# Two places for the maxima over keys, and the value product one step sooner, in a gated cross-attention block on one Trainium2 core

## The chip, the cores and the metric

The kernel runs on 1 core of one Trainium2 chip. The metric is the device time of one execution in microseconds (us). A core has five engines that each work through a queue of their own in order: TensorE (PE in the profile; PEld are its weight loads), VectorE (DVE), ScalarE (ACT), GpSimd (POOL) and SyncE (SP), which here issues most of the DMA transfers. An instruction waits, at the head of its queue, for semaphores that other engines or transfers raise.

## The reference

The inputs are x and a context, 16 x 128 x 1024 in float32 each, two gate scalars and the weights of one block. Cut to what matters:

```python
q = (layernorm(x) @ Wq).reshape(b, s, KV_HEADS, GROUP, HEAD_DIM)      # 8 key heads, groups of 4, 32 wide
k = (ctx @ Wk).reshape(b, s, KV_HEADS, HEAD_DIM)
v = (ctx @ Wv).reshape(b, s, KV_HEADS, HEAD_DIM)
scores = einsum('bqhgd,bkhd->bhgqk', q, k) / sqrt(HEAD_DIM)
out = einsum('bhgqk,bkhd->bqhgd', softmax(scores), v).reshape(b, s, 1024) @ Wo
x = x + tanh(g_xattn) * out
h = silu(layernorm(x) @ W_gate.T) * (layernorm(x) @ W_up.T)           # 2752 wide
x = x + tanh(g_ffn) * (h @ W_down.T)
```

Attention is over the 128 keys of one of the 16 batch elements.

## The kernel before

**Numbers in two parts.** Products are done on pairs of a high part (rounded, type fp32r) and a low part (the rest). `split` makes them: ScalarE copies the source to the high part (line 114), VectorE subtracts it from the source to get the low part (line 115). `mm3` (lines 122 to 124) then multiplies high by high, high by low and low by high.

**The stages.** The 2048 tokens are worked on in two groups of 1024. `projections` makes k, v and q for both groups and writes them to DRAM; `attention` reads them back and works on 64 units per group (one unit is one key head of one batch element: 128 keys against 4 heads x 128 queries, so 512 columns); `Outer` does the product with Wo, the residual and the second layernorm; `Gated` and `Down` are the feed-forward part. The matmuls of these last two are all on line 707.

**Interleaving.** The order is written out by hand: `manual_schedule` keeps each engine's queue in the order in which the program issues. Generators are stepped against each other. The *host* of the first group's attention is `projections`, which yields after every 12 matmuls of 512 columns (about). For each host step `due` grows by RATE = 1.08, and `attention` is stepped once for each whole unit in `due`. So about every twelfth host step is followed by two attention steps at once, a *double step*. The second group's attention runs later with the gated products as its host and has settings of its own.

**One attention step.** With `gap` = 1 a new unit begins at each step. At step i the generator first runs what was put off to this step (`later`: the stores of os, and the reciprocals of the row sums), then in this order `gather`, `scores`, `take`, `rest`, `leave`, `shift`, `expo`, each for unit i minus its lag. The lags of the first group are 0 (scores), 1 (take), 2 (shift), 3 (expo), 4 (rest), 6 (gather), 6 (leave). For unit n they do:
- `scores`, line 472: one matmul into a bank `by` (two places). After every second unit it loads ks and qs for two pairs of units later (lines 451, 465, 466).
- `take`: ScalarE copies the scores to `pr` (line 481, 4 places); GpSimd reduces them to the maximum over the 128 partitions, which are the keys, into `mx` (line 483). `mx` has one place: the pool's default is `bufs=1`.
- `shift`, line 486: VectorE subtracts `mx` from `pr`. It frees `mx`.
- `expo`: ScalarE takes the exponential (line 489) and rounds it to the high part `ph` (line 491, 3 places).
- `rest`, line 495: VectorE makes the low part `pl` = `pr` - `ph` (2 places). It frees `pr`.
- `gather`: two matmuls into a bank `av` (two places), the first with `ph` (line 500), the second with `pl` (line 501). After every second unit it loads the next v (line 458).
- `leave`, line 511: the result goes to `os`, by ScalarE for even units and by VectorE for odd ones, and a step later SyncE stores it (line 515).

The second group calls the same function with nb = 1, lags of its own and another order of the parts.

SyncE's queue holds all of this together with the projections' own transfers: weights (line 168), x (line 218), context (line 188) and the stores of k, v and q (lines 253, 413), in the order of the program.

Of the kernel before, what the change touches and what calls it, by code (L numbers as in the profile page):

```python
# [10 lines left out]
F32 = mybir.dt.float32  # L11
F32R = mybir.dt.float32r
# [5 lines left out]
P = 128  # L18
# [9 lines left out]
TB = 512  # L28
# [26 lines left out]
def flamingo_kernel(ctx: ExitStack, tc: tile.TileContext, x, ctxt, gx, gf, wqkv, wo, wgu, wge, wd, out):  # L55
# [11 lines left out]
    def pool(name, side=None, space=None):  # L67
        kw = {"name": name, "bufs": 1}
        if side:
            kw["side"] = side  # L70
        if space:
            kw["space"] = space
        return tc.tile_pool(**kw)
# [362 lines left out]
    def attention(ap, ps_, cells, gap, lags, npr, nq, nb):  # L436
        units = [(m, j) for m in range(len(cells)) for j in range(2)]
        ks, vs, qs, ss, pr, mx, ph, pl, po = ({} for _ in range(9))
# [40 lines left out]
        def take(n):  # L479
            pr[n] = ap.tile([P, TB], F32, name="pr", tag="pr", bufs=npr)  # L480
            nc.scalar.copy(pr[n], ss.pop(n))  # L481
            mx[n] = ap.tile([P, TB], F32, name="mx", tag="mx")
            nc.gpsimd.partition_all_reduce(mx[n], pr[n], P, bass_isa.ReduceOp.max)  # L483

        def shift(n):
# [1 line left out]

        def expo(n):
            nc.scalar.activation(pr[n], pr[n], AF.Exp, scale=SCALE)
            ph[n] = ap.tile([P, TB], F32R, name="ph", tag="ph", bufs=3)  # L490
            nc.scalar.copy(ph[n], pr[n])

        def rest(n):
# [57 lines left out]
        while i <= last or later:  # L551
            for fn in later.pop(i, []):
                fn()
            for fn in order:
                n = i - steps[fn]
# [17 lines left out]
    class Outer:  # L573
# [38 lines left out]
        def part(self, i, meanwhile=None):  # L612
            raw = self.raw.pop(i)[:, 0]
            self.o[i] = o = stile((i + 1) % 3 if i else 0)
            h, l = (o[:, z].rearrange("p h k t -> p (h k) t") for z in range(2))
            nc.scalar.copy(h, raw)
            if meanwhile:
                meanwhile()
            nc.vector.tensor_tensor(l, raw, f32(h), ALU.subtract)
# [277 lines left out]
    def casts(cb, n):  # L897
        def cast(name, src, k=slice(0, KQ), cols=slice(0, TB)):
            if name not in cb or cb[name] is None:
                cb[name] = mtile(name)  # L900
            c = cb[name]
            kk = slice(k.start, min(k.stop, n))
            split(c[0][:, kk, cols], c[1][:, kk, cols], src[:, kk, cols])

        return cast

    def quarter(mq, i, dtype=F32):

        n = f"q{i // 2}{i % 2}"
        return mq.tile([P, KQ, TB], dtype, name=n, tag=n)  # L910
# [34 lines left out]
    def swap(cb, units, first, mq, n, src, made, early):  # L945

        q = {}

        def load(i, what):
            q[i] = quarter(mq, i)
            nc.sync.dma_start(q[i][:, :n], what())

        def make(name, i):
            cb[name] = None
            casts(cb, n)(name, q[i])

        def bring(name):
            m = cb[name] = mtile(name)  # L960
            for k, z in enumerate(m):
                nc.sync.dma_start(f32(z[:, :n]), made[name][:, k])

        whats = (lambda: src(0, 0), lambda: made["m5"], lambda: src(1, 0), lambda: made["m7"])
        for i, (u, what) in enumerate(zip(early, whats)):
            u.before.append(lambda i=i, what=what: load(i, what))
        u = units[-1]
        u.after[1] = [lambda: (make("m1", 0), load(0, lambda: src(1, 1)))]
        u.after[5] = [lambda: make("m5", 1)]
        u.after[6] = [lambda: bring("m6")]  # L970
        u.after[4] = [lambda: bring("m4")]
        first.after[1] = [lambda: make("m2", 2)]
        first.after[5] = [lambda: make("m7", 3)]
        first.after[6] = [lambda: make("m3", 0)]
# [102 lines left out]
    with ExitStack() as body:  # L1077
        body.enter_context(tc.manual_schedule())
        psB = body.enter_context(pool("psB", None, PSUM))
        cb = {}  # L1080
        o = Outer(0)
        hooks = {
            26: [lambda: o.load(0)],
            28: [lambda: o.added(0)],
            29: [lambda: o.scaled(0)],
            30: [lambda: o.part(0), lambda: o.load(1)],
        }
        with pool("pp", "right") as pp, pool("psP", None, PSUM) as psP:
            pairs = [(t, b) for t in range(2) for b in range(BPB)]
            cells = [(t, c, b) for c in range(2) for t, b in pairs] + [(t, c, b) for t, b in pairs for c in range(2, 4)]  # L1090
            with pool("early", "left") as early:
                host = projections(pp, early, cb, hooks)
                for _ in range(LEAD):
                    next(host)
            with pool("att", "left") as att:
                follow = attention(att, psP, cells, 1, (0, 1, 2, 3, 4, 6, 6), 4, 2, 2)
                due = 0
                for _ in host:
                    due += RATE
                    while due >= 1:  # L1100
                        next(follow, None)
                        due -= 1
                for k, _ in enumerate(follow):
                    if k == 0:
                        o.norm(1)
        mB = body.enter_context(pool("mB", "right"))
        fp = body.enter_context(pool("fp", "right"))
        groups = [[Gated(g, f) for f in range(NFT)] for g in range(NGRP)]
        downs = [[Down(c, p) for p in range(NTOK // (2 * P))] for c in range(len(CHUNKS))]
        tail = groups[1] + sum(downs, [])  # L1110
        for a, b in zip(tail, tail[1:]):
            a.follow = b

        with pool("mq", "left") as mq:
            o.rows(0)
            host = outer(0, cb, lambda: mq, o, groups[0], Edge(0))
            for _ in range(BUSY):
                next(host)
        o = Outer(1)
        with pool("att", "left") as att, pool("psC", None, PSUM) as psC:  # L1120
            cells = [(t, c, b) for t in (2, 3) for b in range(BPB) for c in range(KV // 2)]
            follow = attention(att, psC, cells, 2, (0, 0, 1, 2, 4, 6, 6), 3, 2, 1)
            due, head = 0, len(FIRST) - BUSY
            for k in range(head + 7 * (NFT - 3) + 4):
                due += MORE * (k % 7 == (head + 4) % 7)
                for _ in range(1 + (due >= 1)):
                    next(follow, None)
                due -= due >= 1
                next(host)
            for _ in follow:  # L1130
                pass
        mq = body.enter_context(pool("mq", "left"))
        w = {}

        def fill(z):
            w[z] = quarter(mq, z)
            src = wo[KQ * (z % 2) : KQ * (z % 2) + KQ, :, ts(z // 2, TB)]
            nc.sync.dma_start(w[z], src.rearrange("k p d -> p k d"))

        def turn(z):  # L1140
            cb[QUARTERS[z]] = None
            for k in (0, 2):
                casts(cb, KQ)(QUARTERS[z], w[z], slice(k, k + 2))

        for z in range(4):
            fill(z)
        u = groups[0][-1]
        u.before.append(lambda: (o.rows(0), o.load(0)))
        u.after[5] = [lambda: o.norm(0)]
        u.after[6] = [lambda: turn(0)]  # L1150
        u.after[7] = [lambda: (o.part(0), o.load(1)), lambda: turn(2)]
        u.amid = lambda: turn(1)
        u.after[4] = [lambda: turn(3)]
        for _ in host:
            pass
        for name in ("m1", "m2", "m5"):
            cb[name] = None

        def part(c):
            def src(h, j):  # L1160
                n = len(CHUNKS[c]) // 2
                r = CHUNKS[c][0] * P + h * n * P
                return wd[r : r + n * P, ts(j, TB)].rearrange("(k p) d -> p k d", p=P)

            return src

        before = (groups[1], *downs)
        for c in range(len(CHUNKS)):
            n, made = len(CHUNKS[c]) // 2, {"c": c}
            premake(groups[1][1 + 6 * c :], mq, n, part(c), made)  # L1170
            u = before[c]
            early = (u[-3], u[-3], u[-2], u[-2]) if c == 0 else u[-6:-2]
            swap(cb, u, downs[c][0], mq, n, part(c), made, early)
        for _ in outer(1, cb, lambda: mq, o, tail, Edge(1)):
            pass
# [44 lines left out]
```

## Time and profile before

| | |
|---|---|
| median of 3 runs | 1840.36 us (1840.12 to 1842.83) |
| profiled execution | 1839.81 us, span 1838.0 us |
| TensorE busy | 1816.5 us, 99% of the span |
| VectorE, ScalarE, GpSimd busy | 66%, 49%, 30% |
| first attention, first to last score matmul | 107.1 to 327.7 us |
| GpSimd's maxima (line 483), both groups | 128 of 2157 ns, 276.1 us |
| VectorE's low parts (line 495), both groups | 128 of 945 ns, 121.0 us |

The rows of a timeline are: start in us from the beginning of the span, duration in us, engine, line of the kernel, operation, output <- inputs, and in brackets the idle time of that engine just before and what ended it. A row of waits is: engine, tile and line <- who ended the wait, then us in total, times, longest us. A row on one tile has the shortest, median and longest duration in ns. A row of the stretch table is: window, its length, then busy us (and instructions) of PE, PEld, DVE, ACT, POOL, the granted clock of TensorE, the share of the 16 DMA engines, GB/s.

### The profile page before, as it was taken

To read this page: it belongs to the slowest core of one execution; us is meant where nothing else is said; L and a number is where in the kernel's file an instruction comes from. 1 tells how busy PE (TensorE), PEld (TensorE's weight loads), DVE (VectorE), ACT (ScalarE), POOL (GpSimd) and SP (SyncE) were. 2 spreads that over 40 slices of the span, in tenths; PEclk is the share of its full clock that TensorE was granted. 3 is DMA by queue.
4 is the path that set the end of the run, shared out by engine and by line. 5 is a ranking of instruction groups with operands and counts; after the bars stand their busy time and mean duration, and the time that the engine had idled before them with its cause. 6 is when DMAs were issued, how large, how long until landed. Compare 5 with 4: busy or idle time off the path is not lost.

```text
span 1838.0 us, 23463 instructions
## 1 busy us (share of the span) xinstructions
PE 1816.5 (99%) x8296; PEld 1493.4 (81%) x8296; DVE 1210.6 (66%) x1551; ACT 900.7 (49%) x1301; POOL 546.3 (30%) x372
## 2 busy tenths in 40 slices
PE   9999999999999999999999999999999999999999
PEld 8877877888877777787888888888888888888887
DVE  6758778668877777776578635355356656745765
ACT  4457787435677777776434434333334212312321
POOL 1136566221233333331021233244330231122021
PEclk9999999999999999999999999999999999999999
DMA  9699999774555455543674565675666566665764
GB/s 331 208 274 289 285 285 269 239 258 134 159 146 151 144 148 146 147 138 118 218 252 161 145 204 187 188 210 168 170 206 258 201 233 204 245 215 180 258 201 157
DMA packets 232565, 373.55 MB, mean 203 GB/s; under 512 B 38016, under 2 KB 124288, under 8 KB 227328
## 3 DMA queue, kind: packets, MB, share of 16 engines
q1 hardware_dynamic: 210400, 333.77, 55.7%
q10 hardware_dynamic: 14112, 25.17, 4.6%
q0 software_dynamic: 7936, 13.11, 4.4%
q8 instruction: 66, 1.08, 0.2%
q14 instruction: 51, 0.42, 0.1%
HBM read 247.99 MB, written 122.42 MB: 202 GB/s over the span
## 4 chain that ended last, share of the span: by engine, by line
PE 85%; DVE 5%; DMA 4%; ACT 2%; issue 2%; POOL 1%; SPq 1%; DVEq 0%; POOLq 0%; ACTq 0%
PE bx L707 36%; PE bz L707 18%; PE by L707 9%; PE bz L124 3%; PE bz L122 3%; PE bz L123 3%; PE bx L124 3%; PE bx L123 3%; PE bx L122 3%; PE av L501 1%; DMA od<-os 1%; PE av L500 1%; DVE pl L495 1%; POOL mx L483 1%; DVE pr L486 1%
## 5 line engine op out<-in xcount | busy, mean ns | idle before, releaser
L483 POOL PARTITION_ALL_REDUCE mx<-pr x128 | 276.1, 2157 | 343.4 <-ACT pr L481 167.3
L674 POOL TENSOR_TENSOR sum<-raw 128x512 f32<-128x512 f32 (+1 forms) x37 | 48.0, 1298 | 479.4 <-DVE stc L115 479.4
L114 ACT CAST sta<-raw 128x1024 fp32r<-128x1024 f32 (+1 forms) x66 | 67.7, 1026 | 241.7 <-PE by L707 232.6
L707 PE MATMUL bz<-m5h,stb 128*128 128x512 f32 (+1 forms) x528 | 169.9, 383 | 0.0
L707 PE MATMUL bx<-m4h,std 128*128 128x512 f32 x512 | 168.8, 390 | 1.0 <-DVE c L753 0.8
L707 PE MATMUL bx<-m6h,stb 128*128 128x512 f32 (+1 forms) x528 | 169.6, 383 | 0.0
L707 PE MATMUL bx<-m7h,stc 128*128 128x512 f32 x512 | 168.6, 389 | 0.0
L707 PE MATMUL bz<-m3h,stc 128*128 128x512 f32 x512 | 168.5, 389 | 0.0
L707 PE MATMUL by<-m2h,sta 128*128 128x512 f32 x512 | 168.5, 389 | 0.0
L707 PE MATMUL bx<-m1h,sta 128*128 128x512 f32 x512 | 168.4, 389 | 0.0
L751 DVE TENSOR_TENSOR c<-by,c 128x512 f32<-128x512 f32 x42 | 28.8, 687 | 144.1 <-issue 137.6
L495 DVE TENSOR_TENSOR pl<-pr,ph 128x512 fp32r<-128x512 f32 x128 | 121.0, 945 | 2.2 <-PE av L501 2.2
L144 POOL TENSOR_TENSOR rs__143<-ve,mhalf 128x1 f32<-128x1 f32 x32 | 29.3, 916 | 312.4 <-DVE nm L142 303.0
L851 DVE SCALAR_TENSOR_TENSOR c<-bx,tg,c 128x512 f32<-128x512 f32 x96 | 72.0, 750 | 66.3 <-PE bx L707 62.5
L707 PEld LDWEIGHTS bz<-m5h,stb 128*128 128x128 f32 x528 | 98.2, 188 | 20.2 <-DVE stb L115 0.5
L707 PEld LDWEIGHTS bx<-m6h,stb 128*128 128x128 f32 x528 | 98.4, 188 | 20.0
L707 PEld LDWEIGHTS bx<-m4h,std 128*128 128x128 f32 x512 | 96.1, 188 | 22.6 <-DVE c L753 1.2
L707 PEld LDWEIGHTS bx<-m7h,stc 128*128 128x128 f32 x512 | 96.1, 188 | 20.5 <-issue 0.2
L707 PEld LDWEIGHTS by<-m2h,sta 128*128 128x128 f32 x512 | 96.1, 188 | 20.5
L707 PEld LDWEIGHTS bx<-m1h,sta 128*128 128x128 f32 x512 | 96.1, 188 | 20.4
L707 PEld LDWEIGHTS bz<-m3h,stc 128*128 128x128 f32 x512 | 96.1, 188 | 20.1
L486 DVE TENSOR_TENSOR pr<-pr,mx 128x512 f32<-128x512 f32 x128 | 87.6, 684 | 37.0 <-POOL mx L483 36.7
(400 smaller groups left out, 4635.9 us busy)
## 6 DMA issues: line engine op xcount, KB each, us to landing
raw<-in_wgu SPq DMA_DIRECT2D x42, 1024.0 KB, 6.7
x1d<-c SPq DMA_DIRECT2D x96, 256.0 KB, 2.8
c<-x1d ACTq DMA_DIRECT2D x96, 256.0 KB, 3.0
hd<-c SPq DMA_DIRECT2D x86, 256.0 KB, 2.2
od<-os SPq DMA_DIRECT2D x128, 160.0 KB, 4.0
qd<-e SPq DMA_DIRECT2D x32, 512.0 KB, 5.5
qs<-qd SPq DMA_DIRECT2D x64, 256.0 KB, 4.4
raw<-od SPq DMA_DIRECT2D x32, 512.0 KB, 5.1
```

Source lines behind the costliest of these rows:

```text
L114: nc.scalar.copy(h, src)
L122: nc.tensor.matmul(ps, lh, rh, start=first, stop=False)
L123: nc.tensor.matmul(ps, lh, rl, start=False, stop=False)
L124: nc.tensor.matmul(ps, ll, rh, start=False, stop=last)
L144: nc.gpsimd.tensor_tensor(rs, ve, mhalf, ALU.pow)
L483: nc.gpsimd.partition_all_reduce(mx[n], pr[n], P, bass_isa.ReduceOp.max)
L486: nc.vector.tensor_tensor(pr[n], pr[n], mx.pop(n), ALU.subtract)
L495: nc.vector.tensor_tensor(pl[n], pr.pop(n), f32(ph[n]), ALU.subtract)
L674: lambda: tt(s1, a[1][0], a[1][1], sub),
L707: nc.tensor.matmul(ps, l_, r_, start=start and k == i == 0, stop=k == n - 1 and i == 2, skip_group_check=not start)
L751: tt(c[1], ps, c[1], ALU.add)
L851: nc.vector.scalar_tensor_tensor(y, ps, g, y, ALU.mult, ALU.add)
```

## The change

In the first group (nb = 2) the maxima get two places and the high part `ph` two instead of three. In the second group (nb = 1) both stay as they were. The lags of `gather` and `leave` in the first group go from 6 to 5, so that the value product of unit n stands ahead of the scores of unit n+5 in TensorE's queue, and the copy to os, its store and the next v load move with it.

```diff
         def take(n):
             pr[n] = ap.tile([P, TB], F32, name="pr", tag="pr", bufs=npr)
             nc.scalar.copy(pr[n], ss.pop(n))
-            mx[n] = ap.tile([P, TB], F32, name="mx", tag="mx")
+            mx[n] = ap.tile([P, TB], F32, name="mx", tag="mx", bufs=nb)
             nc.gpsimd.partition_all_reduce(mx[n], pr[n], P, bass_isa.ReduceOp.max)
 ...
         def expo(n):
             nc.scalar.activation(pr[n], pr[n], AF.Exp, scale=SCALE)
-            ph[n] = ap.tile([P, TB], F32R, name="ph", tag="ph", bufs=3)
+            ph[n] = ap.tile([P, TB], F32R, name="ph", tag="ph", bufs=4 - nb)
             nc.scalar.copy(ph[n], pr[n])
 ...
-                follow = attention(att, psP, cells, 1, (0, 1, 2, 3, 4, 6, 6), 4, 2, 2)
+                follow = attention(att, psP, cells, 1, (0, 1, 2, 3, 4, 5, 5), 4, 2, 2)
```

## The prediction

> **What bounds the kernel now.** I read the page first, then TensorE's stretches, then the waits and the timeline of the first attention (100 to 360 us), the only place that the change touches.
>
> ```profile
> PE 1816.5 (99%) x8296; PEld 1493.4 (81%) x8296; DVE 1210.6 (66%) x1551; ACT 900.7 (49%) x1301; POOL 546.3 (30%) x372
> ...
> PE 85%; DVE 5%; DMA 4%; ACT 2%; issue 2%; POOL 1%; SPq 1%; DVEq 0%; POOLq 0%; ACTq 0%
> ```
>
> TensorE (PE) is the bound: work off it counts only where PE stands still. In the timeline, matmuls of 512 columns start 0.227 us apart in a row. What successive starts take beyond that adds up, from 100 to 360 us, to 12.0 us. That is all that can be won. The stretch table shows the worst place:
>
> ```profile
> 270.00:280.00 10.00, 7.54 (x33) 5.41 (x32) 8.32 (x13) 7.26 (x13) 7.30 (x3) 1.00 0.93 290
> 280.00:290.00 10.00, 10.00 (x37) 7.86 (x38) 7.01 (x11) 8.55 (x15) 6.77 (x3) 0.83 0.97 274
> ```
>
> PE is busy 7.54 of 10 us, and in the next row the granted clock (third number from the end) is 0.83. The timeline has the cause, a gap of 2.36 us:
>
> ```profile
> 277.15 0.39 PE L472 MATMUL by<-qs,ks 96*128 96x512 f32 x1
> ...
> 279.91 0.46 PE L500 MATMUL av<-ph,vta 128*80 128x512 f32 x1 [2.36 <-DVE os L511]
> ```
>
> Eight matmuls after it start 0.36 to 0.43 us apart: 1.5 us more. The rest of the 12.0 us: scores that wait for their q load (1.34 us at 178.34, 0.46 at 186.65, 1.04 at 203.57, 1.45 at 213.11), a score that waits for a bank (0.68 at 234.91), and crumbs.
>
> Why the attention is late there: the maxima have one place. Waits of GpSimd (POOL), 100 to 360 us, and a stretch of the timeline, POOL and VectorE (DVE):
>
> ```profile
> POOL mx L483 <- DVE pr L486: 64.4, 51, 5.0
> ```
>
> ```profile
> 257.25 0.67 DVE L486 TENSOR_TENSOR pr<-pr,mx 128x512 f32<-128x512 f32 x1
> ...
> 257.85 1.21 DVE L115 TENSOR_TENSOR wl<-raw,wh 128x1024 fp32r<-128x1024 f32 x1
> ...
> 258.09 3.22 POOL L483 PARTITION_ALL_REDUCE mx<-pr  x1 [1.17 <-DVE pr L486]
> ...
> 258.98 0.68 DVE L495 TENSOR_TENSOR pl<-pr,ph 128x512 fp32r<-128x512 f32 x1
> ...
> 261.34 0.69 DVE L486 TENSOR_TENSOR pr<-pr,mx 128x512 f32<-128x512 f32 x1 [1.68 <-POOL mx L483]
> ```
>
> Each reduce starts 0.17 us after the shift (L486) before it ends, though its input (the copy to pr) lay ready 3.7 us earlier; then DVE stands 1.68 us for the reduce. The two form a ring: reduces start at 254.31, 258.09 and 262.20, so 7.89 us for two units, where PE needs 2 x 3.44 (scores at 248.78, 252.25, 255.69). The ring falls behind by 1 us per pair here.
>
> **The change part by part.** No instruction is added: 64 units keep their counts, and 2 KB per partition go from ph to mx.
>
> *Second place for mx.* The reduce of unit 40 could start when the one before it ends, at 256.92 instead of 258.09. But now shift 39 (due 257.25) runs beside it, which the trace never shows. The nearest row is pl, the same subtraction beside reduces (answers on the tiles mx and ph):
>
> ```profile
> L483 POOL PARTITION_ALL_REDUCE mx<-pr x128: 1783/2080/3220, 111.5 to 848.3; - x128
> ...
> L495 DVE TENSOR_TENSOR pl<-pr,ph x128: 622/684/1573, 120.6 to 860.2; 128x512 fp32r<-128x512 f32 x128
> ```
>
> Its longest is 1573 against 684 ns: 0.89 us lost. So shift 39 ends by 258.8, wl (1.21) and pl (0.68) follow, less overlap, and shift 40 starts at 260.55 instead of 261.34: 0.8 us won per two units. Bounds: 1.68 won (no stretch) to 0.1 lost (two stretches of 0.89). I take 0.8. It matters where the 1.68 waits stand: units 10, 12, 14, 16, 20 and 34, 36, 38, 40, 42, 44, 46.
>
> [...]
>
> *Value product a step sooner.* The value pair (L500, L501) of unit n stands ahead of score n+5 instead of n+6. Its second matmul needs pl of n, which DVE makes in attention step n+4. PE reaches it 0.23 us before the old start of score n+5, plus 0.46 us since one more pair (2 x 0.23) has been issued. Against the ends of pl in the trace, what is too late (with 0.06 us for the signal) is largest at unit 6 (142.60 against 140.91: 1.75 us) and unit 41 (272.50 against 270.13: 2.43). Behind a standing pair on PE's queue wait the next score and 12 projection matmuls.
>
> Worst are the five places where two attention steps follow each other without projections, because pl then has no time between (second scores 9, 22, 36, 49, 63). There units 4, 17, 31, 44, 58 are late by 1.48, 1.26, 1.37, 0.45 and 0.61 us, on top of the trace's own waits. The last of them:
>
> ```profile
> 326.87 0.40 PE L472 MATMUL by<-qs,ks 96*128 96x512 f32 x1
> ...
> 327.22 0.69 DVE L115 TENSOR_TENSOR e<-bx,e 128x512 fp32r<-128x512 f32 x1 [0.70 <-ACT e L114]
> ...
> 327.73 0.50 PE L472 MATMUL by<-qs,ks 96*128 96x512 f32 x1
> ...
> 327.83 0.68 DVE L495 TENSOR_TENSOR pl<-pr,ph 128x512 fp32r<-128x512 f32 x1
> ```
>
> pl starts after the second score already did; it follows an evacuation that waits for PE, so no relief of the ring moves it.
>
> *Two places for ph.* ph of n waits for the first value matmul of n-2, now in step n+3; before, that of n-3, in the same step n+3. No cost; ScalarE waited 0.4 us for it, once. The copies to os (L511) and their stores move with the product; the free bank is asked for at the same distance.
>
> *SyncE's queue.* The v load (L458) moves from just ahead of ks and qs to the attention step before, ahead of the projections' loads and stores. It took SyncE 1.44, 1.11 and 0.93 us just ahead of the q loads for 186.65, 203.57 and 213.11, whose scores started 0.09 to 0.13 us after the landing. So of 0.46, 1.04 and 1.45 us some 0.5 stays: 2.4 us won. Bounds: nothing (the DMA engines' share is about 1.0 there, so landing may not move) to 2.95.
>
> Summed by stretch, against the same run:
> - to score 22: unit 4's 1.5 us stands where the trace waits for the q load anyway, and the ring's five waits (5 x 0.8) cover units 6 to 17: 0 (-0.4 to +1.3).
> - 22 to 30: -2.4 (-2.95 to 0).
> - 31 to 50: 1.37 us at unit 31, where DVE waits for ScalarE's casts and the ring wins nothing. That delay and some 4 us from the ring cover unit 41. At 44 PE then arrives at 277.15 + 0.46 + 1.37 + 0.46 = 279.44, and score 49 starts at 279.67 instead of 280.43 + 0.46: -1.2. Without the gap of 2.36 us the slow matmuls go too: -1.5. Units 48 and 49, late by 0.3 on the old times, take 0.4 back: -2.3 (-3.7 to +0.5).
> - 51 to the end: units 58 and 63 (late by 0.44): +1.0 (0 to +1.1).
>
> Sum -3.7 us (-7.0 to +2.9). The profiled execution took 1839.81 us (span 1838.0 and 1.81 around it), 0.55 under the median of 1840.36; on the median -3.7 gives 1836.6. That is just beyond 0.2% (3.7 us), about what a measurement of this kernel can tell from no change.
>
> [...]
>
> **The rivals.**
> *The double steps decide (slower).* If reduce n+1 takes its input ahead of shift n each time, two shifts lose 0.89 each: 7.89 - 1.68 + 1.78 = 7.99 us per pair, no relief. PE now has one step of lead over DVE instead of two, and where DVE's work is tied to PE each stall is paid anew: 1.48 + 1.26 + 1.37 + 0.45 + 0.61 + 0.44 = 5.6 us. At unit 17 the gap grows to 1.58 + 1.26 = 2.84 us, over the 2.36 that cost 1.5 us of clock: +7.1, 1847.5. It decides if pl of 17 and 41 come less than about 1 us sooner. For it: the ring's 0.89 is a maximum from few cases; against: most pl that a reduce holds up take 0.93, a loss of 0.24. 0.26.
> *The ring was all (much faster).* No shift is stretched (1.68 won per pair), all q waits go, unit 31 costs nothing: -7.0, 1833.4. For it: reduces have 1.78 us as minimum and 3.4 us room; against: unit 31 waits for ScalarE. 0.20.
> *Nothing gained:* q waits stay, since landing is bound by the DMA engines: -3.7 + 2.4 = -1.3, 1839.1; I count it into the forecast case's spread.
>
> **How the numbers follow.** The forecast case (0.54) lies around -3.7, half on each side of the 0.2% bound: 0.27 faster, 0.27 same. With 0.20 from the much faster rival, faster is 0.47; slower is 0.26. The range reaches from just under the much faster rival, 1832.5, to just under the slower one's full price, 1847.0. The forecast case alone: 1834 to 1841.
>
> **What would show it.** In the profile after: POOL's wait for DVE's shift (64.4 us) falls below 20; no gap at 280 and no clock below 1.00 there; value matmuls (L501) waiting for pl at five places, about 1 us each; q waits near 204 and 213 gone or halved; shift's longest over 684 ns. The prediction is wrong if L501's waits for pl add up to more than 8 us, or a new clock dip appears.

## The result, and the profile after

The changed kernel takes 1848.26 us (median of 6 runs, 1843.15 to 1851.53) against 1840.53 for the kernel before beside it: ratio 1.0037, 95% interval 1.0023 to 1.0050. It is slower by 7.7 us, where 3.7 us less were forecast. The profiled execution took 1848.77 us, span 1847.0.

The page after, the two lines that were shown of before:

```profile
PE 1818.5 (98%) x8296; PEld 1496.2 (81%) x8296; DVE 1228.6 (67%) x1551; ACT 901.0 (49%) x1301; POOL 549.4 (30%) x372
...
PE 86%; DMA 6%; DVE 3%; ACT 3%; issue 1%; SPq 0%; ACTq 0%; DVEq 0%
```

Counts are the same. VectorE is busy 18 us longer, and in the chain DMA rose from 4 to 6%. The sum that the prediction made (what successive matmul starts take beyond their usual distance, 100 to 360 us) rose from 12.0 to 16.8 us. Of the other 4.2 us between the two profiled spans, most stands in the feed-forward part (1040 us to the end: 0.7 before, 4.8 after), where the runs below have 0.5 to 4.2 whatever their edit; 2.60 us of it is one gap at 1585.3, and e10 has one like it (2.98 us at 1577.6). I count it as spread, which is not shown for this kernel.

The ring is gone as forecast. Waits of POOL, 100 to 360 us, and the row of the shift (shortest, median and longest ns):

```profile
POOL mx L483 <- ACT pr L481: 84.6, 46, 14.6
POOL mx L483 <- DVE pr L486: 12.8, 10, 2.1
```

```profile
L486 DVE TENSOR_TENSOR pr<-pr,mx x64: 671/678/1533, 114.8 to 341.1; 128x512 f32<-128x512 f32 x64
```

The wait for the shift fell from 64.4 to 12.8 us; now the reduce waits for ScalarE's copy, its input. The price is there too: the longest shift took 1533 ns (695 before). And here is what PE waits for instead, 100 to 360 us:

```profile
PE av L501 <- DVE pl L495: 7.5, 5, 1.9
PE av L500 <- DMA vta<-vd: 3.7, 2, 3.4
```

The q waits near 178, 187, 204 and 213 us are gone, all of them. In their place five second value matmuls wait for pl: of units 4, 6, 17, 31 and 58 (delays of 1.28, 0.89, 2.08, 1.98 and 2.08 us). All but that of unit 6 stand at double steps. Unit 17 in the timeline:

```profile
178.44 0.40 PE L472 MATMUL by<-qs,ks 96*128 96x512 f32 x1
...
178.68 0.40 PE L500 MATMUL av<-ph,vta 128*80 128x512 f32 x1
178.79 0.69 DVE L115 TENSOR_TENSOR e<-bz,e 128x512 fp32r<-128x512 f32 x1 [0.60 <-ACT e L114]
...
179.34 1.78 POOL L483 PARTITION_ALL_REDUCE mx<-pr  x1 [2.87 <-ACT pr L481]
179.40 1.52 DVE L495 TENSOR_TENSOR pl<-pr,ph 128x512 fp32r<-128x512 f32 x1
...
180.98 0.46 PE L501 MATMUL av<-pl,vta 128*80 128x512 f32 x1 [1.90 <-DVE pl L495]
```

PE has issued the first matmul of the pair 0.24 us after the first score of the double step. pl can only start after an evacuation (lines 114 and 115, which take a finished projection out of its bank), and since the reduce now starts as soon as its input is there, pl runs beside it and takes 1.52 us (0.93 for this unit before). The median of pl in the first group rose from 683 to 922 ns.

The place at 280 us is worse than it was. Stretches, then the timeline:

```profile
270.00:280.00 10.00, 9.72 (x42) 7.13 (x40) 8.09 (x13) 7.58 (x14) 7.13 (x4) 1.00 0.99 299
280.00:290.00 10.00, 6.84 (x23) 5.38 (x24) 4.85 (x9) 5.59 (x10) 4.91 (x3) 0.83 1.07 296
```

```profile
275.43 0.43 PE L500 MATMUL av<-ph,vta 128*80 128x512 f32 x1
...
275.70 0.64 SPq L458 DMA_DIRECT2D vta<-vd  x1
...
279.40 0.40 PE L472 MATMUL by<-qs,ks 96*128 96x512 f32 x1
...
283.15 0.43 PE L500 MATMUL av<-ph,vta 128*80 128x512 f32 x1 [3.35 <-DMA vta<-vd]
```

The product of unit 44 is now the second of this double step, and it waits 3.35 us for its v: issued at 275.70, landed at 283.02. SyncE came to it 3.7 us after PE had started the last product from that place (271.98): its queue had stood 2 us (269.85 to 271.88) issuing a store of os whose copy had ended at 268.61 (why that took so long no run shows), and six more issues lay between. The product of unit 42 at 275.43 had waited for its v load too (landed at 275.29), by 0.24 us. The load of unit 44 also took longer: issued at almost the same time as before (275.61), it landed after 7.32 us instead of 3.90. No run here shows why.

### The profile page after: what moved, and what is told of

Read it like the earlier page. It is cut to its first block, busy times and chain, and to the rows that moved or that the text cites. A ratio compares the mean times of both kernels' runs of the same rounds, so it can differ in the third digit from the quotient of the medians.

```text
span 1847.0 us, 23480 instructions
## 1 busy us (share of the span) xinstructions
PE 1818.5 (98%) x8296; PEld 1496.2 (81%) x8296; DVE 1228.6 (67%) x1551; ACT 901.0 (49%) x1301; POOL 549.4 (30%) x372
## 4 chain that ended last, share of the span: by engine, by line
PE 86%; DMA 6%; DVE 3%; ACT 3%; issue 1%; SPq 0%; ACTq 0%; DVEq 0%
PE bx L707 34%; PE bz L707 17%; PE by L707 8%; PE bz L124 4%; PE bz L122 4%; PE bz L123 4%; PE bx L123 4%; PE bx L124 4%; PE bx L122 3%; DMA od<-os 2%; PE av L501 1%; PE av L500 1%; DMA vta<-vd 1%; DMA c<-x1d 1%; PE by L472 1%
## 5 line engine op out<-in xcount | busy, mean ns | idle before, releaser
L495 DVE TENSOR_TENSOR pl<-pr,ph 128x512 fp32r<-128x512 f32 x128 | 132.6, 1036 | 0.1
L115 DVE TENSOR_TENSOR stb<-sum,stb 128x1024 fp32r<-128x1024 f32 (+1 forms) x66 | 79.5, 1204 | 44.1 <-ACT stb L114 44.1
```

What stands on the lines that cost most here:

```text
L115: nc.vector.tensor_tensor(l, src, f32(h), ALU.subtract)
L495: nc.vector.tensor_tensor(pl[n], pr.pop(n), f32(ph[n]), ALU.subtract)
```

## The experiments

Sixteen experiments ran (e13 and e16 repeat the kernels of e8 and e9). The table has the median, the ratio to the kernel before, run beside it, with its 95% interval, PE's lost time in the profiled execution (100 to 360 us, as above) and what of it I put down to three causes: waits of L501 for pl, waits of scores (L472: q loads, banks, pr), and waits of L500 (v, or a bank that a copy to os holds). Before: 12.0; 0.2, 5.5, 2.8. After: 16.8; 8.3, 0, 4.3.

| run | median us | ratio [95%] | lost | pl | scores | L500 |
|---|---|---|---|---|---|---|
| e1 after, mx one place | 1846.19 | 1.0036 [1.0020, 1.0053] | 15.8 | 9.2 | 0.7 | 3.1 |
| e2 sooner product alone | 1844.72 | 1.0028 [1.0018, 1.0038] | 17.4 | 9.8 | 0.8 | 3.7 |
| e3 mx two, ph two, lag 6 | 1845.93 | 1.0040 [1.0026, 1.0054] | 15.8 | 0 | 7.7 | 5.0 |
| e4 mx two, os two, lag 6 | 1851.00 | 1.0059 [1.0042, 1.0075] | 22.0 | 1.2 | 8.1 | 7.3 |
| e5 mx two alone | 1840.07 | 1.0001 [0.9991, 1.0011] | 10.7 | 0.3 | 3.6 | 4.5 |
| e6 partner of e5, mx one | 1839.91 | 0.9997 [0.9987, 1.0007] | 12.0 | 0 | 3.8 | 5.0 |
| e7 after, v three places | 1844.01 | 1.0022 [1.0012, 1.0031] | 13.8 | 9.7 | 1.1 | 0 |
| e8 after, no double steps | 1835.05 | 0.9979 [0.9966, 0.9992] | 3.9 | 2.9 | 0 | 0 |
| e9 before, no double steps | 1839.54 | 0.9997 [0.9987, 1.0007] | 9.4 | 0 | 6.8 | 1.2 |
| e10 as e8, v three places | 1838.60 | 0.9997 [0.9985, 1.0009] | 7.7 | 4.6 | 0.7 | 0 |
| e11 before, ph two | 1850.28 | 1.0056 [1.0043, 1.0069] | 20.8 | 0.7 | 9.3 | 5.3 |
| e12 before, os two | 1853.96 | 1.0081 [1.0068, 1.0095] | 24.8 | 1.4 | 10.2 | 7.9 |
| e13 as e8, again | 1837.27 | 0.9983 [0.9969, 0.9998] | 5.9 | 3.9 | 0.9 | 0 |
| e14 e2, no double steps | 1838.31 | 0.9985 [0.9975, 0.9995] | 7.5 | 5.6 | 0.5 | 0 |
| e15 e5, no double steps | 1836.00 | 0.9972 [0.9960, 0.9984] | 11.9 | 0.2 | 6.8 | 1.1 |
| e16 as e9, again | 1839.82 | 0.9994 [0.9983, 1.0004] | 12.4 | 0 | 6.6 | 1.5 |

A profile is of one run: in e4, e15 and e16 of the longest, in e1, e7, e9 and e11 of the shortest of that kernel's runs. Besides e15 and e10, what the lost time differs by from before and what the median differs by agree within 3 us.

**The change taken apart (e1 to e4).** My first theory A was that the lost lead costs and mx wins a part back; C that shifts beside reduces cost; B that two places for ph cost.

e1, the change without the second place for mx:

```diff
-            mx[n] = ap.tile([P, TB], F32, name="mx", tag="mx", bufs=nb)
+            mx[n] = ap.tile([P, TB], F32, name="mx", tag="mx")
```

> The change with one place for mx (ph in two places and the value product a step sooner stay). Before and after are 1840.5 and 1848.3 us. Theory A (the lost step of lead costs, the second place for mx wins part of it back): slower than after, 1850 to 1860, with GpSimd's waits for the shift back above 50 us between 100 and 360 us and more than the 7.5 us that TensorE waited for pl in after. Theory C (the shift beside the reduce is what costs): faster than after, 1838 to 1843.

e2, the same with ph in three places, so the sooner product alone (edit to e1):

```diff
-            ph[n] = ap.tile([P, TB], F32R, name="ph", tag="ph", bufs=4 - nb)
+            ph[n] = ap.tile([P, TB], F32R, name="ph", tag="ph", bufs=3)
```

> The sooner value product alone (mx in one place, ph in three, as before). If two places for ph cost nothing, as the prediction said, within 1.5 us of e1. Theory B (the second place taken from ph costs): at least 3 us faster than e1. Theory A: 1850 to 1860 as e1; theory C: 1838 to 1843.

e3, the change with the product at its old place (edit to the changed kernel):

```diff
-                follow = attention(att, psP, cells, 1, (0, 1, 2, 3, 4, 5, 5), 4, 2, 2)
+                follow = attention(att, psP, cells, 1, (0, 1, 2, 3, 4, 6, 6), 4, 2, 2)
```

> mx and ph in two places each, the value product left at six steps. ph then waits for a product one step later than in after, so ScalarE gets a wait of its own. Theory A: no wait of TensorE for pl at the double steps; 1836 to 1842, the low end if ScalarE's wait is short. Theory C: 1845 to 1850.

e4, the kernel before with mx in two places, and os in two instead of three for room:

```diff
-            mx[n] = ap.tile([P, TB], F32, name="mx", tag="mx")
+            mx[n] = ap.tile([P, TB], F32, name="mx", tag="mx", bufs=nb)
 ...
-            os_ = ap.tile([VW, G, P], F32, name="os", tag="os", bufs=2 * nb - 1)
+            os_ = ap.tile([VW, G, P], F32, name="os", tag="os", bufs=2 if nb == 2 else 1)
```

> The second place for mx alone; its 2 KB come from os, which has two places instead of three. Theory A: 1833 to 1837 (the waits for q loads and the gap at 280 us of before go, TensorE waits for pl under 2 us in the window), unless the stores from os hold ScalarE up. Theory C: 1845 or more.

e1 and e2 lie between the ranges of A and C and bear out neither. The sooner product alone (e2) brings most of the loss; its interval and that of the change overlap. Two places for ph at lag 5 (e1 against e2) show nothing: the intervals overlap widely. But e3 and e4, which A wanted faster than before, are slower, as C had it, with few or no waits for pl (0 and 1.2 us). Either C was right or something else was in them.

**What was wrong with e3 and e4 (e11, e12).** The same two savings of room in the kernel before, with mx in one place: ph in two places (e11), and os in two (e12).

> The kernel before with ph in two places and nothing else. With the product at lag 6, ph of n then waits for the product of n-2, which stands one attention step later in the program. Theory P (this, not mx, made e3 slow): 1844 to 1848. Theory C (in e3 the second mx did it): 1840 to 1842.

> The kernel before with os in two places and nothing else, the control of e4. Theory O (the third place of os, given up for room, made e4 slow): 1847 to 1852. Theory C (in e4 the second mx did it): 1840 to 1843.

Both are slower than before without a second mx, even by more than P and O had put them: the room given up was the cost. By the ratios they lie 2.9 and 4.0 us above their partners with two mx, e3 and e4; the intervals overlap. In e11 ScalarE waits for the value product before it can round to ph, and holds up its copies (ACT waits, 100 to 360 us, e11, then before):

```profile
ACT ph L491 <- PE av L500: 27.5, 30, 2.8
```

```profile
ACT ph L491 <- PE av L500: 0.4, 1, 0.4
```

At lag 6 the product of n-2 stands one attention step later than the rounding of n. So ph needs three places there, and two only with the sooner product: the change's second and third edit belong together. In e12 the copies to os wait 23.0 us for stores on ScalarE and 11.4 on VectorE (9.2 and 0.2 before).

**The second place for mx by itself (e5, e6).** Room came from writing pl into its own pr. Scores and exponentials of the first group are rounded in both for that, and pl is zero.

```diff
-            pr[n] = ap.tile([P, TB], F32, name="pr", tag="pr", bufs=npr)
+            pr[n] = ap.tile([P, TB], F32 if nb == 1 else F32R, name="pr", tag="pr", bufs=npr)
 ...
-            mx[n] = ap.tile([P, TB], F32, name="mx", tag="mx")
+            mx[n] = ap.tile([P, TB], F32, name="mx", tag="mx", bufs=nb)
 ...
-            pl[n] = ap.tile([P, TB], F32R, name="pl", tag="pl", bufs=2)
+            pl[n] = ap.tile([P, TB], F32R, name="pl", tag="pl", bufs=2) if nb == 1 else pr[n]
 ...
-                follow = attention(att, psP, cells, 1, (0, 1, 2, 3, 4, 6, 6), 4, 2, 2)
+                follow = attention(att, psP, cells, 1, (0, 1, 2, 3, 4, 6, 6), 5, 2, 2)
```

> The second place for mx by itself, with the product at lag 6, three places for ph and three for os: room for it is made by writing pl into its own pr (which then has five places, and pl none of its own). For that pr is of the rounded type in the first group, so scores and exponentials are rounded there and pl is zero; the instructions are the same in number and size. Theory A (the ring of one mx holds the chain up, so a second place wins): at least 2 us under its partner e6 and 1834 to 1838. Theory C (shift and rest then run beside reduces and lose what the ring won): within 1.5 us of e6 or above it, 1839 to 1846.

e6 is e5 with mx in one place.

> Partner of e5: the same low part in place and the same rounding, mx in one place as in the kernel before. Both theories: pr in five places that live until the value product is about as long as before, so 1838 to 1842.

1.0001 against 0.9997: no difference, which is what theory C gave, though not for its reason (the median of pl is 683 ns in e5 and 682 in e6), and though the ring is relieved (waits of POOL and VectorE, 100 to 360 us, e6, then e5):

```profile
POOL mx L483 <- DVE pr L486: 67.0, 52, 5.4
DVE pr L486 <- POOL mx L483: 33.2, 29, 1.7
```

```profile
POOL mx L483 <- DVE pr L486: 13.4, 11, 1.7
DVE pr L486 <- POOL mx L483: 2.8, 2, 1.7
```

The gap at 280 us stays (2.25 us in e6, 2.96 in e5), and the timeline of e5 has who holds it:

```profile
279.26 0.58 ACT L511 COPY os<-av 80x512 f32<-80x512 f32 x1 [1.95 <-DMA od<-os]
...
279.89 0.71 PE L500 MATMUL av<-ph,vta 128*80 128x512 f32 x1 [2.96 <-ACT os L511]
```

By the profile the product waits for a copy to os that frees a bank, and the copy for the store that has the place of os. A faster ring moved none of these here.

**The v load (e7).** The change with v in three places:

```diff
-        vta = [ap.tile([P, 2, VW], F32R, name=f"vta{i}") for i in range(2)]
+        vta = [ap.tile([P, 2, VW], F32R, name=f"vta{i}") for i in range(2 + (gap == 1))]
 ...
-                vs[m] = vta[m % 2]
+                vs[m] = vta[m % len(vta)]
 ...
-                load_v(m + 2)
+                load_v(m + len(vta))
 ...
-        for m in range(2):
+        for m in range(len(vta)):
```

> The change with v in three places instead of two, each loaded three pairs ahead. Theory V (the v load that PE waits for at 283 us is a cost by itself): its 3.5 us and the slow matmuls behind it (1.7 us) go: 1842.5 to 1845. Theory S (the product stands too close behind pl, and what one stall gives up the next takes): the waits for pl grow and the time is 1846.5 to 1849.

The waits for v are gone, and the mean granted clock of the profiled execution is 0.999 instead of 0.997; 1844.01 lies in what theory V gave. By the ratios this took off 2.8 us, by the medians 4.3, of the 7.7; the intervals of e7 and the change overlap. The waits for pl stay, 9.7 us.

**The double steps (e8, e9, e10).** e8 is the change with one attention step to each step of the projections, started four steps sooner:

```diff
-LEAD = 27
-RATE = 1.08
+LEAD = 23
+RATE = 1.0
 ...
-                    at_step(0, QS + 3 + i, lambda b=b: (stats(n + b), xs.pop(n + b)))
+                    at_step(0, QS + 3 + i // 2, lambda b=b: (stats(n + b), xs.pop(n + b)))
```

> The change with no double steps: RATE 1.0 and LEAD 23, so that attention is stepped once for each step of the projections and starts four steps sooner (the statistics of the second group's x move with it). Theory D (the waits for pl stand at the double steps): the waits of L501 for pl, 7.5 us after the change, fall under 2 us, the first dip of the clock goes too, and the time is 1838 to 1842.5. Theory S: under half of the 7.5 us goes, and the time is over 1845.

e9 makes the same edit in the kernel before, e10 in e7.

> The kernel before with no double steps (RATE 1.0, LEAD 23), the partner of e8. Theory D (the sooner product is only dear where pl has no time between two steps): without double steps the sooner product and the second mx cost nothing or win, so this stands at 1834 to 1839, e8 at or under it. Theory E (the sooner product costs some us everywhere): this is at least 3 us under e8, 1829 to 1832.

> The change without double steps and with v in three places. In e8 no wait for a v load over 0.25 us is left, so theory D: the third place wins nothing more, 1833 to 1837, the same as e8. If the v load also slowed what the waits do not show: under 1832.

PE's waits in e8 (100 to 360 us) and the stretch that had the gap of before and that of after:

```profile
PE av L501 <- DVE pl L495: 2.2, 4, 1.1
```

```profile
270.00:280.00 10.00, 10.00 (x45) 7.98 (x44) 7.56 (x11) 8.43 (x14) 6.43 (x4) 1.00 0.98 304
280.00:290.00 10.00, 10.00 (x45) 7.91 (x45) 9.63 (x13) 9.20 (x16) 7.52 (x4) 1.00 1.11 296
```

Without double steps the change is faster than before instead of slower, by more than theory D had put it (2.2 us of waits for pl are left, where it allowed 2), and no v is late. The kernel before gains nothing by the same edit (e9, just above D's range), so it is the sooner product together with the old stepping that is dear. The edit also starts the attention some 10 us sooner (first score at 97.0 instead of 107.4) and moves the second group's statistics; no run parts these from the double steps. That the double steps do it rests on the trace, where four of the five waits for pl stood. e10 was to equal e8 and lies at 0.9997; its runs spread from 1830.98 to 1844.50 and its interval overlaps e8's, so it settles nothing.

**Both parts without double steps, on one chip (e13 to e16).** e13 is e8's kernel and e16 e9's; e14 and e15 are e2 and e5 with the edit of e8.

> The change without double steps (the kernel of e8), now on one chip with its partners. Theory D (the double steps alone made the change dear): 1833 to 1837 and at least 2.5 us under e16. If e8 was luck of the runs: within 1.5 us of e16.

> The sooner value product alone (mx in one place, ph in three), without double steps. Theory F (the sooner product wins by its v and q loads' place in SyncE's queue): close to e13, 1834 to 1837. Theory G (with one mx the chain stays behind and pl comes too late for lag 5): 1839 to 1844, with waits of L501 for pl over 3 us.

> The second place for mx alone (product at lag 6, pl in place and rounded as in e5), without double steps. Theory F: as e16, 1838 to 1841, with the q waits of e9 still there. Theory H (the second mx is what wins): 1833 to 1837.

> The kernel before without double steps (the kernel of e9): 1838 to 1841 by every theory, as in e9.

e13 stands at 0.9983, 2.55 us under e16, at the edge of what theory D wanted; the two intervals overlap a little. e14 (0.9985) and e15 (0.9972) are also faster than before. e14 lies between the ranges of F and G. e15 lies 3.8 us under e16 and in the range of H, the second mx as the winner; their intervals hardly touch. But e15 also has pl in place and rounded, and its partner with one mx and no double steps was not run, so H is not shown. Which part wins how much, the times don't resolve: the medians lie within 4 us while single runs spread over 10. The traces do show the trade. With the product at lag 5 (e8, e13, e14) scores lose 0 to 0.9 us and pl costs 2.9 to 5.6; at lag 6 (e9, e15, e16) scores lose 6.6 to 6.8 and pl 0.2 at most. e14, with one mx, has the most waits for pl.

e8 with e13, e14, and e15 with its coarser rounding beat both kernels; e15 by 0.28% [0.16, 0.40].

## Why the prediction was wrong

The forecast case failed, and the rival "the double steps decide", given 0.26, came out: it was priced at 1847.5, and 1848.26 was measured. That the price fits so well is luck in part. Between 100 and 360 us PE's lost time rose by 4.8 us, not by the rival's 7.1: waits for pl by 8.1 (5.6 in the rival's sum), waits of L500 by 1.5 and the rest by 0.7, less 5.5 for scores; that sum had no late v, and it left the q waits standing. The other 4.2 us between the two profiles lie outside.

The starts of the same scores, before and after, give the prediction's own stretches. From the difference I take 0.26 us that the first score started late, and 0.46 for the one pair more that PE has issued by then:

| stretch | forecast (range) us | measured us |
|---|---|---|
| to score 22 (178.34, after 181.28) | 0 (-0.4 to +1.3) | +2.2 |
| 22 to 30 (213.11, after 214.52) | -2.4 (-2.95 to 0) | -1.5 |
| 30 to 50 (285.48, after 288.70) | -2.3 (-3.7 to +0.5) | +1.8 |
| 50 to 63 (327.73, after 332.93) | +1.0 (0 to +1.1) | +2.0 |
| sum | -3.7 (-7.0 to +2.9) | +4.5 |

So three of the four stretches failed, the third by most: there the gap of 2.36 us and its slow matmuls were to go, and a wait of 3.35 us for v with slow matmuls of its own came. Step by step:

*Second place for mx.* The mechanism held (POOL's wait for the shift under 20 us, the longest shift stretched) and the size of the stretch too: 1533 against 678 ns is 0.86 us, where I took 0.89. The failed step is the next: "It matters where the 1.68 waits stand". VectorE's wait was relieved (33.2 us in e6, 2.8 in e5), and with the double steps in place PE gained nothing. Nor did the relief reach pl where the sum spent it: pl of unit 6 ended at 142.77 us (142.60 before) and that of unit 17 at 180.92 (179.77 before). At 280 us I laid PE's gap to the ring because the trace named VectorE's copy to os; in e5 the gap stands without the ring's waits, and the profile puts a copy there behind its store. The -1.2 and -1.5 us of that stretch did not come by the ring. In the kernel before itself that copy stood behind VectorE's own work (the store of unit 38, whose place it takes, had landed at 273.77), so that stores would have held the gap there too is concluded from e5, not shown. I had also put the stretch on the shift alone; it falls on pl as well, and at a double step pl is what PE waits for.

*Value product a step sooner.* The places were right: of the double steps' units 4, 17, 31, 44 and 58, four waited for pl, and 44 for v. The sizes were not. Unit 58 was put at 0.61 and took 2.08; its pl ran 1.27 us beside a reduce. Worse was the sum over stretches. Unit 4's 1.48 was written off against a q wait, and unit 6's 1.75 and unit 17's 1.26 against the ring's relief; 1.28, 0.89 and 2.08 us were paid. This term was in the sum with 1.37 + 0.4 + 1.0 us; the runs have 8.3 us (8.3 to 9.8 in after, e1, e2 and e7).

*SyncE's queue.* Right in direction and too small: the scores lost 5.5 us before (0.7 of it for a bank) and nothing after, where I took 2.4. (The 1.44 us given there for the load ahead of 186.65 belong to the next v load, at 185.45; the one ahead took 0.46, and the sum stays.) That q loads do come sooner shows in e8 against e9, where PE is hardly late: the one for unit 24 landed at 180.23 instead of 183.54. In the changed kernel PE's own lateness has a part in it: the q load for unit 28 landed 1.3 us later than before, but PE came 2.9 us later. But the step asked only what the moved load does to q. It did not ask for the load's own slack, which stood in the trace of before as 2.7 and 5.5 us (landing to product) for the pairs of units 42 and 44. With the product 3.4 us sooner against the scores and a double step between, they fell to 0.14 and 0.13; for unit 44, 3.4 us of that is the longer way of the load. e7 puts the price at 3 to 4 us.

*Two places for ph.* Right: nothing (e1, e2), and e11 shows why the two edits have to come together.

*The clock.* I allowed one slow stretch to vanish; instead two stand in the first attention (granted clock 0.50 from 181.66 and from 284.06 us), after the waits of units 17 and 44. The rival saw the first.

Of the signs of being wrong that I had written down, waits for pl over 8 us or a new dip, the dips came; the view of waits sums these waits to 7.5 us.

## What to carry to other kernels

A consumer moved one step closer to its producer is priced at the tightest step of the schedule, here the steps that come in pairs, and not at the mean distance: one unit of lead was worth 5 to 7 us of waits for q and banks, and cost 8 to 10 us of waits for pl, 3 to 6 once the pairs were spread out. When an edit moves a load, compute the new slack of that load itself, to its own reader, before asking whom it makes room for. And a wait may be written off against a relief only when the relief has been followed to the instruction that is waited for.

## What the runs showed of the hardware

In the profile of the changed kernel TensorE's granted clock is 0.50 in three stretches, from 181.66, 284.06 and 669.77 us, each 3.41 us long. Their starts lie 102.40 and 385.71 us apart, 30 and 113 times 3.413 us. Cut into cells of this length, counted from these starts, the profile gives (columns as in the stretch table):

```profile
178.25:181.66 3.41, 1.51 (x8) 0.86 (x7) 2.87 (x4) 3.27 (x7) 1.78 (x1) 1.00 1.02 363
181.66:185.07 3.41, 3.41 (x14) 3.03 (x12) 2.11 (x4) 2.70 (x5) 2.27 (x2) 0.50 1.17 288
232.86:236.27 3.41, 2.75 (x12) 1.78 (x11) 3.26 (x5) 3.41 (x7) 1.95 (x2) 1.00 0.81 228
236.27:239.69 3.42, 2.27 (x10) 1.92 (x11) 3.42 (x6) 3.24 (x6) 2.85 (x2) 1.00 0.97 315
239.69:243.10 3.41, 3.41 (x17) 2.71 (x16) 3.15 (x4) 2.74 (x6) 1.58 (x2) 1.00 1.11 274
```

The gap of 1.90 us before 180.98 lies in one cell (PE busy 1.51) and the next cell runs at 0.50. The gap of 1.81 us before 237.42 is cut by a cell's edge (2.75 and 2.27 busy), and nothing follows; nor does anything after the gap of 1.91 us before 332.63, which an edge cuts too (2.28 and 2.63 busy). So in this profile the time that PE stood in one cell tells more than the length of the gap. In the profiles of before and after together, from the first matmul to the last, the cells in which PE stood 1.82 (666.36 us, after), 1.90 (178.25, after), 2.36 (277.10, before) and 2.51 us (280.65, after) were followed by one at 0.50. One with 1.85 was not (1581.13, after; the gap of 2.60 us before 1585.3, cut by an edge), nor was any other, all with 1.44 us or less. In the stretch from 284.06 us matmuls of 512 columns start 0.427 us apart instead of 0.227, so eight of them take 1.6 us more. Gaps of 1.8 to 2.6 us brought that cost in these two profiles or did not, as the edges fell; that this is one source of the spread is a guess, which no run shows.

GpSimd's reduces take 1.78 us at the least. The longest pl took 1573 ns (before, beside a reduce), 0.89 us over its median of 684; the longest shift took 1533 (after, beside a reduce), and in e8 and e5 1533 and 1535. In the profiles of before and after every shift and every pl over 0.80 us ran beside a reduce, and none without one beside it took over 0.70. In turn the longest reduce of the first group grew from 3.22 us before to 4.34 after; VectorE was busy 4.23 us of it (130.75 to 135.09).
